# Pair products on one core: weight loads by the software queue alternate between 14 and 15 DMA engines, dealt from one place further on

## The chip, the cores and the metric

The kernel runs on one core of a Trainium2 chip. The metric is the device time of one execution in microseconds (us): the median of the runs shown, and beside it one execution taken with the hardware profiler.

## The reference

An input x has 1024 rows, 32 fields and 128 values a field; there is one 128 x 128 weight matrix for each of the 496 pairs of fields i < j. For each pair, field i's values go through the pair's matrix, and the result is multiplied, element by element, with field j's values:

```python
v_i = inputs[:, I_IDX, :]
v_j = inputs[:, J_IDX, :]
transformed = jnp.einsum('bpd,ped->bpe', v_i, W)
return transformed * v_j
```

All is float32. The output has 1024 x 496 x 128 elements, 260 MB; the inputs are 49 MB together. So the kernel writes five times what it reads.

## The kernel before

The 496 pairs are worked off in one order, written out by hand in the loop of line 300: each step u is a half pair, 512 of the 1024 rows. Pairs stand from the last first field to the first, so that fields are needed one after the other. The order in the program is the order on each engine; there is no scheduler.

For a half pair, TensorE makes two products (line 268) of a split of x and of the weights into parts with fewer bits, ScalarE scales the sum (line 270), TensorE adds a third product (line 279), and VectorE multiplies with the other field from PSUM into an output slot (line 244). The first 15 pairs use plain float32 products (line 265). Weights are split in chunks of two pairs by `split_w` (lines 149 to 153: ScalarE, then three GpSimd instructions), x by `split_x`.

Stores are issued on ScalarE's queue (line 318), three or four pairs at a time, 1.5 or 2 MB in rows of 12 or 16 KB per partition. `slots` has room for 12 pairs; until the x fields that need it are loaded, the room of those fields holds output too (`ot`). VectorE has to wait for a slot's store to be done before it writes there again.

Weights come in tiles of eight pairs, 128 partitions x 4 KB = 512 KB, 62 of them. Three tiles have room at a time; when the last chunk of a tile is split, the loop (line 324) loads the tile three further on into its place. SyncE issues most of the loads (line 132). From tile 12 on, every second tile (`WAPART`: 12, 14, ... 60, 25 tiles) is loaded in two parts by `load_apart`:

- the first 112 partitions by the software queue, issued on GpSimd (line 114). The source is written as 14 x 8 rows, and the host has laid the tile's rows out in that order, so that the DMA falls into 14 pieces of eight rows of 4 KB;
- the last 16 partitions by SyncE (line 115), a row for each of the 16 DMA engines.

`move_on(k)` (line 111) is a DMA of the same software queue that reads 2k rows of 64 bytes as k pieces into a tile, `mark`, that nobody reads. It is called with 5 once before the loads begin (u = 30), with 16 - 14 = 2 three pairs after each load (`BACK`), and with 13 after the last one. The numbers sum up to 5 + 25 x 14 + 24 x 2 + 13 = 416 = 26 x 16.

Of the kernel before, what the change touches and what calls it, by code (L numbers as in the profile page):

```python
# [11 lines left out]
P = 128  # L12
# [5 lines left out]
WL = 8  # L18
# [12 lines left out]
XLEAD = 5  # L31

XG = 4
NE = 14
ROWS = 8 * NE
WAPART = tuple(range(12, 62, 2))
BACK = 3
FOURS = 73
NS = 12
# [18 lines left out]
def kernel(  # L58
# [22 lines left out]
    nc = tc.nc  # L81
# [12 lines left out]
    def load_x(f, pieces=1, eng=None):  # L94
        if f == 0:

            t = rpool.tile([P, WL, P], F32, tag="w", name="x_0").rearrange("p q e -> p (q e)")
        else:
            t = xpool.tile([P, BT], F32, tag=f"x{f}", name=f"x_{f}")
        s = BT // pieces  # L100
        for k in range(pieces):
            (eng or nc.sync).dma_start(out=t[:, k * s : (k + 1) * s], in_=xt[f, :, k * s : (k + 1) * s])
        x_sb[f] = t

    w_raw = {}
# [3 lines left out]
    def move_on(k):  # L109

        nc.gpsimd.dma_start(out=mark[: 2 * k], in_=xt[0, : 2 * k, :16].rearrange("(b a) n -> a b n", a=k))

    def load_apart(dst, src):
        nc.gpsimd.dma_start(out=dst[:ROWS], in_=src[:ROWS].rearrange("(b a) m n -> a b m n", a=NE))
        nc.sync.dma_start(out=dst[ROWS:], in_=src[ROWS:])

    group = {}

    def load_group(k, m):
        if m == XG - 1:  # L120
            group[k] = xpool.tile([P, XG, BT], F32, tag=f"g{k}", name=f"x_g{k}")
        f = XG * k + 1 + m
        x_sb[f] = group[k][:, m, :]
        nc.sync.dma_start(out=x_sb[f], in_=xt[f])

    def load_w(c, splits=(0, WL), eng=nc.sync):
        w_raw[c] = rpool.tile([P, WL, P], F32, tag="w", name=f"w_{c}")
        if c in WAPART:
            load_apart(w_raw[c], wt[c])
            return  # L130
        for a, b in zip(splits, splits[1:]):
            eng.dma_start(out=w_raw[c][:, a:b, :], in_=wt[c, :, a:b, :])
# [59 lines left out]
    todo.sort(key=lambda t: t[1])  # L192

    load_w(0, (0, 1, WL), nc.sync)
    load_x(NF - 2, pieces=2, eng=nc.scalar)
    load_x(NF - 1, pieces=2, eng=nc.scalar)
    load_x(NF - 3)
    load_x(NF - 4)
    load_w(1, eng=nc.sync)
    for f in range(NF - 5, NF - 4 - XLEAD, -1):  # L200
        load_x(f)
    load_w(2, eng=nc.sync)


# [3 lines left out]
        if c < WRING:  # L208
            w_at[max(c * WL - 3 * WC + 1 - WLEAD, free)] = c

    back = []
    last = NQ // WL
    ring = [*range(WRING - WB, XAFTER + 1), "x", *range(XAFTER + 1, last)]

# [42 lines left out]
    def first(u):  # L257
        q, h = divmod(u, 2)
        i, c = pairs[q][0], q // WC
        r = slice(q % WC * P, (q % WC + 1) * P)  # L260
        s = slice(h * HB, (h + 1) * HB)
        if h == 0:
            po[q] = po_t[q % PB]
        if q < nq0:
            nc.tensor.matmul(po[q][:, s], w_raw[q // WL][:, q % WL, :], x_sb[i][:, s], start=True, stop=True)  # L265
        else:
            for t in (0, 1):
                m = nc.tensor.matmul(po[q][:, s], w_s[c][t][:, r], x_s[i][t][:, s], start=t == 0, stop=t == 1)  # L268
                apart(m, scaled.get(u - 1) if h else None)
            scaled[u] = nc.scalar.mul(po[q][:, s], po[q][:, s], 1.0 + EPS)  # L270
            apart(scaled[u], taken.get(q - PB), "TensorE's products, which this waits for, have waited for it")

    def second(u):
        q, h = divmod(u, 2)
        i, j = pairs[q]
        r = slice(q % WC * P, (q % WC + 1) * P)
        s = slice(h * HB, (h + 1) * HB)
        if q >= nq0:
            m = nc.tensor.matmul(  # L279
                po[q][:, s], w_s[q // WC][2][:, r], x_s[i][2][:, s], start=False, stop=True, skip_group_check=True  # L280
            )
            apart(m, scaled[u ^ 1])
        g, k = group_of[q]
        if k == 0 and h == 0:
            ots[g] = out_tile(g)
        if q >= NQ - 2:
            write(g, k, s, po[q][:, s], x_sb[j][:, s])
        elif h == 1:
            taken[q] = write(g, k, slice(0, BT), po.pop(q), x_sb[j])
        ot = ots[g][0]  # L290
        n = groups[g][1]
        if q >= NQ - 2:
            stores.append((u + SLAG, rows(g)[:, k, s], ot[:, k, s]))
        elif g in (0, len(groups) - 1):
            if h == 1:
                stores.append((u + SLAG, rows(g)[:, k], ot[:, k]))
        elif k == n - 1 and h == 1:
            stores.append((u + SLAG, rows(g), ot))

    for u in range(2 * NQ + LAG + SLAG):  # L300
        q = u // 2
        if u < 2 * NQ:
            i, j = pairs[q]
            if u % 2 == 0 and j == i + 1 and XG * ngroup < i - 2 - XLEAD:
                load_x(i - 2 - XLEAD)
            first(u)
            if u == 2 * nq0:
                move_on(5)
            if u % 2 == 0 and q in group_at:
                load_group(*group_at[q])  # L310
            if u % 2 == 1 and q in w_at:
                load_w(w_at[q])
            if u % 2 == 0 and q in back:
                move_on(16 - NE if max(w_raw) < WAPART[-1] else 13)
        if LAG <= u < 2 * NQ + LAG:
            second(u - LAG)
        while stores and stores[0][0] <= u - LAG:
            nc.scalar.dma_start(*stores.pop(0)[1:])
        if u % 2 == 1:
            ready = [t for t in todo if t[0] <= q]  # L320
            if ready:
                ready[0][2](u)
                todo.remove(ready[0])
        if ring[WB:] and ring[0] in spent:
            ring.pop(0)
            c = ring[WB - 1]
            if c == "x":
                load_x(0)
            else:
                load_w(c)  # L330
            if c in WAPART:
                back.append(q + BACK)
        while later and later[0][0] <= u:
            nc.vector.tensor_tensor(*later.pop(0)[1:], ALU.subtract)  # L334
    assert not todo and not later and not stores
# [31 lines left out]
```

## Time and profile before

| | |
|---|---|
| median of three runs | 746.08 us (744.96 to 748.08) |
| the profiled execution | 741.81 us |
| its span, first to last instruction | 739.9 us |
| busy: PE / DVE / ACT / POOL | 703.9 / 637.3 / 634.0 / 595.0 us |
| mean granted TensorE clock | 0.989 |
| moved by DMA | 310.02 MB, mean 419 GB/s |
| store of 1.5 MB, of 2 MB from `slots`, issue to landing | 12.6, 16.5 us |
| software load of 448 KB, issue to landing | 11.6 us |
| SyncE's 64 KB of the same tiles | 6.0 us |

PE is TensorE, DVE VectorE, ACT ScalarE, POOL GpSimd and SP SyncE. The profile's page gives busy time by engine and by line, 40 equal slices of the span with the share of time that the 16 DMA engines were busy, the DMA queues (q10 carries what ScalarE issues, q1 what SyncE issues, q0 the software queue), and who waited for whom. A line such as "A <- B: 29.6, 30, 6.2" says that A waited for B for 29.6 us in all, 30 times, 6.2 us at the longest. The trace behind it has every DMA packet with its queue, start, duration and size, but not the engine that moved it.

### The profile page before, as it was taken

The numbers are of one execution on the slowest core, as the hardware profiler recorded it, in microseconds if no ns is written. First come the engines' busy times: TensorE is split into PE (matmuls) and PEld (weight loads), VectorE is DVE, ScalarE is ACT, GpSimd is POOL, SyncE is SP. The second block draws the span as 40 slices with busy tenths as digits, with TensorE's granted clock in tenths as the row PEclk, the third lists the DMA queues.
The fourth block names the chain that finished last, engine by engine and source line by source line (L and its number), as shares of the span: only waits on it lengthen the run. The fifth ranks groups of instructions, "written<-read, shape, count | busy, mean of one in ns | idle before, by whom it ended". The sixth has DMA issues, their size and how long they took to land.

```text
span 739.9 us, 10346 instructions
## 1 busy us (share of the span) xinstructions
PE 703.9 (95%) x2946; PEld 550.4 (74%) x2946; DVE 637.3 (86%) x550; ACT 634.0 (86%) x1256; POOL 595.0 (80%) x882
## 2 busy tenths in 40 slices
PE   7999999999999999999899979999999999999994
PEld 3577777878778888776688758886778887777782
DVE  3898999999999999988798868987999988997884
ACT  1298999999999999998899968998989999898892
POOL 1789999999999999987789776988787888797660
PEclk9999999999999999999999999999999999999997
DMA  9999999999999999999999999999999999999998
GB/s 346 422 429 423 430 413 429 426 418 428 423 421 428 421 426 424 427 418 426 425 427 424 428 425 406 419 424 425 424 425 419 423 421 421 426 416 424 423 430 330
DMA packets 36968, 310.02 MB, mean 419 GB/s; under 512 B 5552, under 2 KB 5680, under 8 KB 19120
## 3 DMA queue, kind: packets, MB, share of 16 engines
q10 hardware_dynamic: 21888, 261.11, 83.6%
q1 hardware_dynamic: 10592, 36.77, 12.4%
q0 software_dynamic: 4432, 11.48, 4.0%
q8 instruction: 24, 0.39, 0.2%
q14 instruction: 32, 0.26, 0.1%
HBM read 49.29 MB, written 260.05 MB: 418 GB/s over the span
## 4 chain that ended last, share of the span: by engine, by line
PE 60%; DMA 22%; DVE 8%; POOL 3%; ACT 3%; issue 2%; ACTq 0%; DVEq 0%; POOLq 0%
PE po L268 38%; DMA out_dram<-slots 20%; PE po L279 18%; DVE slots L244 5%; PE po L265 4%; ACT po L270 2%; DVE xd L334 2%; DMA out_dram<-ot 1%; DVE ot L244 1%; POOL wd L153 1%; POOL wl L151 1%; POOL xl L168 1%; DMA x<-in_xt_dram 1%; POOL xl L169 0%; POOL wd L152 0%
## 5 line engine op out<-in xcount | busy, mean ns | idle before, releaser
L270 ACT ACTIVATE po<-po 128x512 f32<-128x512 f32 x962 | 553.3, 584 | 74.0 <-PE po L268 57.4
L268 PE MATMUL po<-xh,wh 128*128 128x512 f32 x962 | 382.0, 397 | 17.3 <-DVE slots L244 15.2
L279 PE MATMUL po<-xd,wd 128*128 128x512 f32 x962 | 376.4, 391 | 4.8 <-DVE xd L334 2.4
L268 PE MATMUL po<-xl,wl 128*128 128x512 f32 x962 | 377.2, 392 | 1.2 <-POOL wl L151 0.9
L244 DVE TENSOR_TENSOR slots<-po,x 128x1024 f32<-128x1024 f32 (+1 forms) x263 | 314.0, 1213 | 56.3 <-DMA out_dram<-slots 21.1
L268 PEld LDWEIGHTS po<-xh,wh 128*128 128x128 f32 x962 | 181.2, 188 | 74.0 <-DVE slots L244 30.8
L151 POOL TENSOR_TENSOR wl<-w,wh 128x256 fp32r<-128x256 f32 x241 | 184.8, 767 | 63.6 <-ACT wh L149 57.9
L279 PEld LDWEIGHTS po<-xd,wd 128*128 128x128 f32 x962 | 181.2, 188 | 45.0 <-DVE slots L244 3.2
L268 PEld LDWEIGHTS po<-xl,wl 128*128 128x128 f32 x962 | 181.3, 189 | 40.7 <-POOL wl L151 3.9
L153 POOL TENSOR_TENSOR wd<-wl,wd 128x256 fp32r<-128x256 f32 x241 | 180.3, 748 | 20.1
L244 DVE TENSOR_TENSOR slots<-po,x_g 128x1024 f32<-128x1024 f32 x123 | 148.4, 1223 | 22.3 <-DMA out_dram<-slots 8.5
L244 DVE TENSOR_TENSOR ot<-po,x 128x1024 f32<-128x1024 f32 x99 | 119.4, 1221 | 13.6 <-PE po L279 2.6
L152 POOL TENSOR_SCALAR wd<-wh 128x256 fp32r<-128x256 f32 x241 | 103.5, 429 | 20.5
L149 ACT ACTIVATE wh<-w 128x256 fp32r<-128x256 f32 x241 | 98.6, 410 | 5.7 <-DVE slots L244 5.7
L334 DVE TENSOR_TENSOR xd<-xh,xl 128x512 fp32r<-128x512 f32 x52 | 48.0, 924 | 0.0
L168 POOL TENSOR_TENSOR xl<-x_g,xh 128x512 fp32r<-128x512 f32 x32 | 41.6, 1300 | 2.2 <-ACT xh L167 2.0
L168 POOL TENSOR_TENSOR xl<-x,xh 128x512 fp32r<-128x512 f32 x20 | 25.8, 1292 | 15.8 <-ACT xh L167 15.6
L169 POOL TENSOR_SCALAR xl<-xl 128x512 fp32r<-128x512 f32 x52 | 34.4, 662 | 4.6
L265 PE MATMUL po<-x,w 128*128 128x512 f32 x60 | 29.5, 650 | 4.1 <-DMA x<-in_xt_dram 4.1
L265 PEld LDWEIGHTS po<-x,w 128*128 128x128 f32 x60 | 12.1, 207 | 20.7 <-issue 14.5
L167 ACT ACTIVATE xh<-x 128x512 fp32r<-128x512 f32 x20 | 12.3, 624 | 11.5 <-DMA x<-in_xt_dram 11.4
L167 ACT ACTIVATE xh<-x_g 128x512 fp32r<-128x512 f32 x32 | 20.0, 624 | 0.0
(8 smaller groups left out, 49.5 us busy)
## 6 DMA issues: line engine op xcount, KB each, us to landing
out_dram<-slots ACTq DMA_DIRECT2D x67, 1536.0 KB, 12.6
out_dram<-slots ACTq DMA_DIRECT2D x44, 2048.0 KB, 16.5
out_dram<-ot ACTq DMA_DIRECT2D x28, 2048.0 KB, 12.7
w<-in_wt_dram SPq DMA_DIRECT2D x36, 512.0 KB, 10.9
w<-in_wt_dram POOLq DMA_DIRECT2D x25, 448.0 KB, 11.6
x_g<-in_xt_dram SPq DMA_DIRECT2D x16, 512.0 KB, 16.3
x<-in_xt_dram SPq DMA_DIRECT2D x14, 512.0 KB, 9.4
out_dram<-slots ACTq DMA_DIRECT2D x5, 512.0 KB, 8.9
```

The source lines that it names most:

```text
L149: halved[c] = nc.scalar.mul(h, raw, 1.0 - 2.0**-13)
L151: nc.gpsimd.tensor_tensor(l, raw, h.bitcast(F32), ALU.subtract)
L152: nc.gpsimd.tensor_scalar(d, h.bitcast(F32), EPS, 1.0, ALU.mult, ALU.mult)
L153: nc.gpsimd.tensor_tensor(d, l.bitcast(F32), d.bitcast(F32), ALU.subtract)
L168: nc.gpsimd.tensor_tensor(l, x_sb[f][:, s], h.bitcast(F32), ALU.subtract)
L169: nc.gpsimd.tensor_scalar(l, l.bitcast(F32), 1.0 / EPS, 1.0, ALU.mult, ALU.mult)
L244: i = nc.vector.tensor_tensor(ot[:, k, s], p, f, ALU.mult)
L265: nc.tensor.matmul(po[q][:, s], w_raw[q // WL][:, q % WL, :], x_sb[i][:, s], start=True, stop=True)
L268: m = nc.tensor.matmul(po[q][:, s], w_s[c][t][:, r], x_s[i][t][:, s], start=t == 0, stop=t == 1)
L270: scaled[u] = nc.scalar.mul(po[q][:, s], po[q][:, s], 1.0 + EPS)
L279: m = nc.tensor.matmul(po[q][:, s], w_s[q // WC][2][:, r], x_s[i][2][:, s], start=False, stop=True, skip_group_check=True)
L334: nc.vector.tensor_tensor(*later.pop(0)[1:], ALU.subtract)
```

## The change

The tiles loaded apart alternate: 12, 16, ... keep 14 pieces by the software queue, and 14, 18, ... take 15 pieces of eight rows (120 partitions). A 14-tile's last 16 rows still come by SyncE with the load. A 15-tile's last eight rows come by the software queue too, written as eight rows of two halves, at the place of the mark (`load_rest`, three pairs later), and ahead of it. The mark after a load moves on by 16 less the pieces of the next load (1 or 2), after the last by 12; the first mark has 6 instead of 5. The sum is 6 + 13 x 14 + 12 x 15 + 12 x 1 + 12 x 2 + 12 = 416 again, without the eight-row DMAs.

```diff
-NE = 14
-ROWS = 8 * NE
-WAPART = tuple(range(12, 62, 2))
+WAPART = {c: 14 + k % 2 for k, c in enumerate(range(12, 62, 2))}
+WLAST = max(WAPART)
...
-    def load_apart(dst, src):
-        nc.gpsimd.dma_start(out=dst[:ROWS], in_=src[:ROWS].rearrange("(b a) m n -> a b m n", a=NE))
-        nc.sync.dma_start(out=dst[ROWS:], in_=src[ROWS:])
+    def load_apart(c):
+        n = WAPART[c]
+        dst, src = w_raw[c], wt[c]
+        nc.gpsimd.dma_start(out=dst[: 8 * n], in_=src[: 8 * n].rearrange("(b a) m n -> a b m n", a=n))
+        if n == 14:
+            nc.sync.dma_start(out=dst[8 * n :], in_=src[8 * n :])
+
+    def load_rest(c):
+        if WAPART[c] == 15:
+            a, b = [t[120:].rearrange("a (b m) n -> a b m n", b=2) for t in (w_raw[c], wt[c])]
+            nc.gpsimd.dma_start(out=a, in_=b)
+        move_on(12 if c == WLAST else 16 - WAPART[c + 2])
...
             if u == 2 * nq0:
-                move_on(5)
+                move_on(6)
...
             if u % 2 == 0 and q in back:
-                move_on(16 - NE if max(w_raw) < WAPART[-1] else 13)
+                load_rest(back[q])
...
             if c in WAPART:
-                back.append(q + BACK)
+                back[q + BACK] = c
```

On the host, the rows of a 15-tile are laid out for 15 x 8 instead of 14 x 8.

## The prediction

> **What bounds the kernel now.** I read the page's slices first, then the busy time by stretches, then the queues and the waits.
>
> ```profile
> DMA  9999999999999999999999999999999999999998
> q10 hardware_dynamic: 21888, 261.11, 83.6%
> q1 hardware_dynamic: 10592, 36.77, 12.4%
> q0 software_dynamic: 4432, 11.48, 4.0%
> ```
>
> All 40 slices have the DMA engines at 90% or more, and the three queues sum to 100.0% of 16 engines: the output (q10) takes 84%, the loads by SP (q1) 12%, the software queue (q0), which the change touches, 4%.
>
> ```profile
> 20.00:126.00 106.00, 101.81 (x407) 75.29 (x405) 97.11 (x85) 85.09 (x172) 93.20 (x128) 1.00 1.01 426
> 126.00:697.00 571.00, 554.81 (x2379) 444.17 (x2380) 502.76 (x433) 517.46 (x1028) 480.95 (x720) 0.99 1.01 423
> 697.00:728.00 31.00, 29.80 (x131) 24.01 (x129) 26.91 (x24) 27.50 (x54) 16.93 (x27) 1.00 1.00 426
> 728.00:740.00 12.00, 1.52 (x3) 0.58 (x3) 2.61 (x5) 0.00 (x0) 0.00 (x0) 0.61 0.70 283
> ```
>
> The columns are busy time of PE, weight load, DVE, ACT and POOL, granted clock, DMA share and GB/s. From 20 to 728 us the DMA share is full; compute ends at 732.1, and the last 6 us are stores alone. PE's 95% are stretched by waits for room:
>
> ```profile
> DVE slots L244 <- DMA out_dram<-slots: 29.6, 30, 6.2
> PEld po L268 <- DVE slots L244: 30.8, 40, 5.8
> PE po L268 <- DVE slots L244: 15.2, 18, 5.4
> POOL wl L151 <- ACT wh L149: 57.9, 66, 8.0
> PEld po L268 <- POOL wl L151: 3.9, 8, 1.2
> ```
>
> DVE waits for stores to leave their slots, and PE for DVE. So a store counts as gone when its slowest DMA engine is done, and the time is the work of the DMA engine that has most of it. That needs the engines one by one. The trace's packets carry no engine number, but an engine starts its next packet about 4 ns before the one ahead ends (a 16 KB packet takes 611 ns and the next starts 607 after it), so packets can be strung into 16 chains. Where two chains end within a few ns they may swap names, so I use a chain only for some 16 us around each software load. Three readings:
>
> 1. From 20 to 728 us the 16 chains are idle for 22 engine-us of 11,328: nobody has slack, and who gets 1 us more ends 1 us later. Their last packets end between 735.3 and 738.5 us, 736.4 in the mean.
> 2. In the 17 loads where it can be read cleanly, two chains have no 4 KB packet of q0, only one-row and 4-byte ones, and the following mark DMA falls on just these two. The marks' 128-byte packets (66 = 5 + 24 x 2 + 13) say the same: a software DMA of k pieces uses k engines in turn, and the next goes on behind. Counted from where the kernel begins, the first mark takes engines 0 to 4, each load 5 to 15 and 0 to 2, and each small mark 3 and 4. Engines 3 and 4 are passed over 25 times.
> 3. These two are the slow ones. One (A) needs 25 to 50 ns more than 611 for nearly every 16 KB store from 30 us on, that is 33 ns lost per us, before any weight load by software, and about 0.49 us more around each load. The other (B) loses nothing before 126 us, and then 1.23 us around each load (stores of 700 to 760 ns instead of 611), in two bursts: while the software load runs and at the start of SP's next one. The 14 others lose about 0.13 us a load. I can't tell which of 3 and 4 is A.
>
> Being passed over pays for this: a load costs a taking engine 8 rows and one of SP's 16, 9 x 155 = 1.40 us net; a passed one a row and 8 small packets, 155 + 8 x 5 = 0.20. The difference, 1.20 us a load, 30.0 us in all, meets A's loss (33 ns x 710 us + 25 x 0.49 = 35.7 us) and B's (25 x 1.23 = 30.8), against some 3.3 for the others plus instruction fetches.
>
> **The change part by part.** Load number 1, 3, ... (13 of them) stay at 14 engines; 12 go to 15. Starting at 6 instead of 5, a 14-load takes 6 to 15 and 0 to 3 and passes 4 and 5; one place on, a 15-load takes 5 to 15 and 0 to 3 and passes only 4. So 4 is passed over always, 5 thirteen times, and **3 never**. A 15-load costs a taker 8 rows and one 2 KB piece, 8 x 155 + 80 = 1.32 us, a passed one 0.12. Over 25 loads (before: takers 34.9, passed 4.9 us):
>
> - engine 3: 13 x 1.40 + 12 x 1.32 = 34.0, so +29.1 us
> - engine 4: 13 x 0.20 + 12 x 0.12 = 4.0, so -0.9 us
> - engine 5: 13 x 0.20 + 12 x 1.32 = 18.4, so -16.5 us
> - the 13 others: 34.0, so -0.9 us
>
> The bytes are the same, so nothing is won in the sum; 29 us of one engine are shared out among others that can't use them, since a store waits for the last engine. Engine 3 is A or B, and ends now at about 735 to 736 us by its place among the store landings before 700 us (both at or up to 2 us ahead of the median). With 29.1 more it ends at 764 to 765 instead of 738.5: **+26 us**, if it stays as slow as it is. If the added slowness around a load comes from being passed over, an engine that takes part loses 0.13 instead of 0.49 (A) or 1.23 (B): A gives back 9 us, ending at +17; B 27.5, leaving +1.6 on an engine that has as much slack. No row shows a slow engine taking part, so these are the two ends.
>
> Small edits: 12 more DMA issues on POOL at 632 ns (row L111) are 7.6 us, hidden in POOL's 57.9 us of waiting for ACT above; uncovered, they would lengthen the 3.9 us that PE waits for POOL, at most to 11.5. SP drops 12 issues of 327 ns, off the path. The last 8 rows of a 15-tile now come behind the mark's place, 2.7 us after the load's issue (149.03 and 151.69), and land at most 13.2 us later (longest mark); the tile is split 18 pairs, about 26 us, after its load, so 10 us cover it. Uncovered, ACT's split would wait, with the scaling of products queued behind it and PE behind that. The extra halves of rows (96 packets more at 5 ns) are nothing. The 12 new software DMAs of 0.6 us themselves might each start a burst as a load does; at 1.23 us on one engine that is up to 15 us more on a slow one, which the top of the range takes in part.
>
> [...] The 66 packets show k engines for k pieces when k is the outermost size. [...] No run here shows a k of 1.
>
> **The rivals.** *B is engine 3 and is slow only because it is passed over.* For it: B loses nothing in 96 us before the first software load. Against it: B's second burst comes during SP's ordinary load, in which it is not passed over; and other engines that wait for their turn in a load lose 3 to 20 ns a store where B loses 50 to 120. Then B's +1.6 is covered, all others save 0.9, and the time is 744 to 747, the same.
>
> *Faster.* The same mechanism at its limit: engine 3 is B and gives back all of its 27.5 us, which over 16 engines is 1.7 us, and engine 3's turn in the loads evens out the ends (last 738.5, mean 736.4) for up to 2.1: 3.8 us, 742.3. It decides only if engine 3 gives back 27 of its 29 us or more; each us short of that, past its slack, is a us on the end.
>
> *The place doesn't move as written* (a mark of 1 takes two engines): 3 never, 4 only once passed over; both slow engines carry 28 to 29 us more: 771 to 775.
>
> **How the numbers follow.** The profiled execution took 741.81 us with a span of 739.9, and the median shown is 746.08; I add differences to the median. Forecast, engine 3 left without cover: between +17 (A, giving back) and +26 (A or B as now), nearer to the second, which is how both behave in every row: +24, **770 us**. Chances: as now 0.42, A giving back 0.15, drift 0.09, so slower 0.66; the same 0.28; faster 0.06. A measurement of this kernel tells about 0.5%, 3.7 us, from no change. The range runs from 744 (the same, with its gain of 2 us) to 775 (drift, or a few bursts more); little over 1 in 10 lies outside. The slower case alone: 762 to 775.
>
> **What would show it.** Right: the DMA share falls below 1.00 between 126 and 697 us, to about 0.97, GB/s from 423 to some 410; waits of DVE for out_dram grow from 29.6 by about 20 us; landings of a store stretch, one engine ending it alone by several us; the last stores trail on one engine. Wrong: the share stays at 1.01 with 423 GB/s and the chains still end within 4 us; then B was slow by being passed over. The drift would show in mark packets: q0 has 6 + 12 + 24 + 12 = 54 packets of 128 bytes if a mark of 1 takes one engine, and 42, with 24 of 64 bytes beside them, if it takes two.

## The result, and the profile after

The changed kernel takes **758.0 us** (median of 4 runs, 757.05 to 758.37) where the kernel before takes 745.52 (4 runs, 743.99 to 748.08): ratio **1.0163**, interval 1.0126 to 1.02. (A ratio here is that of the record's comparison of runs in the same state, and not exactly the quotient of two medians.) It is slower, as forecast, but by 12.5 us and not by 24. The profiled execution took 757.05 us, its span is 755.2; against the profiled execution before that is 15.2 us more.

The page's slices and queues, after:

```profile
DMA  9999999999999999999999989999999999999996
q10 hardware_dynamic: 21888, 261.11, 82.5%
q1 hardware_dynamic: 10208, 35.98, 12.0%
q0 software_dynamic: 4816, 12.27, 4.4%
```

The DMA engines are still the bound. The last slice is new: 6 where there was an 8. By stretches (busy PE, weight load, DVE, ACT, POOL, granted clock, DMA share, GB/s):

```profile
20.00:126.00 106.00, 101.90 (x409) 75.51 (x408) 97.29 (x85) 85.64 (x172) 93.39 (x129) 1.00 1.01 427
126.00:697.00 571.00, 545.86 (x2319) 432.71 (x2318) 488.44 (x423) 505.29 (x1002) 478.23 (x717) 0.99 1.00 414
697.00:728.00 31.00, 30.28 (x133) 24.52 (x132) 26.35 (x23) 27.86 (x56) 20.68 (x33) 1.00 1.00 417
728.00:740.00 12.00, 12.00 (x54) 9.94 (x53) 10.78 (x10) 10.85 (x21) 5.64 (x9) 1.00 0.93 384
740.00:756.00 16.00, 2.35 (x8) 1.06 (x7) 4.14 (x6) 1.37 (x3) 0.00 (x0) 0.71 0.56 226
```

Until the first software load (126 us) nothing has changed. From then to 697 us the rate falls from 423 to 414 GB/s. The share of 1.00 in this row is a mean over 571 us, and hides a stretch in which the engines stand idle. From 440 to 455 us, first before, then after:

```profile
440.00:455.00 15.00, 13.27 (x47) 10.77 (x48) 11.68 (x11) 9.26 (x18) 6.08 (x11) 0.77 1.00 406
440.00:455.00 15.00, 9.06 (x34) 7.07 (x33) 7.03 (x7) 6.58 (x13) 6.72 (x11) 0.77 0.75 306
```

Here the stores go over from four pairs to three, and in both kernels VectorE waits over 6 us for a slot; for 11 to 12 us no store is issued (434.3 to 445.6 us before, 441.8 to 453.6 after). The trace has 16 landings for each store. Before, half of those of the store issued at 429.0 us have come 14.7 us later, and the last 1.5 us after that: the engines have work for the gap. After, half of those of the store issued at 430.7 have come 8.0 us later, and the last 9.8 us after that: most engines run dry, and 0.25 x 15 = 3.75 us of each engine's time are lost in the mean. The last landing of a store trails the median by up to 10.6 us ahead of the gap, by 3.9 behind it, then by up to 7.7 again; before, by 3.0 at most.

Past 728 us the share falls again. The stores issued from 728 us on land on 15 engines within 0.1 us or so of their median, except one or two, and on one engine 4.5 to 5.8 us later; from 749.9 to 753.5 us a single engine works. (Before, the 16 ended between 735.3 and 738.5.) Idle engines are not all: the packets from 20 us on take 11,689 us of engine time in place of 11,578, 7 us for each engine. Part of that lies in the executions compared: the one before is near the fast end of its kind (see e12 below).

The waits:

```profile
POOL wl L159 <- ACT wh L157: 65.6, 70, 8.2
PEld po L276 <- DVE slots L252: 39.7, 55, 6.4
DVE slots L252 <- DMA out_dram<-slots: 30.9, 31, 6.8
PE po L276 <- DVE slots L252: 18.9, 22, 5.9
DVE ot L252 <- DMA out_dram<-ot: 7.2, 4, 4.6
PEld po L276 <- POOL wl L159: 5.8, 10, 1.2
```

And before, beside the lines shown in the prediction:

```profile
DVE ot L244 <- DMA out_dram<-ot: 2.1, 4, 0.9
```

VectorE waits 1.3 us more for stores out of `slots` (29.6 before) and 5.1 more for `ot` (2.1). TensorE's waits for VectorE's slots grow by 8.9 (30.8) and 3.7 (15.2). Most of the time, then, VectorE hardly feels an engine that trails by 5 to 10 us. The lag is paid where the other engines have run out of stores: in the gap at 440 us, and at the end.

**The place drifts.** q0's mark packets are 42 of 128 bytes and 24 of 64, the number that the forecast named for a mark of 1 that takes two engines. Strung into chains as in the prediction, the first loads read so (A is the chain that loses some 20 ns on nearly each 16 KB store):

- load 1, 14 pieces: A and one neighbour have no 4 KB packet. The 64-byte packets of the mark behind it are not on these two but on two chains that took part with eight rows.
- load 2, 15 pieces and eight rows: A has nine rows. The next mark of 2 falls on A and one other chain.
- load 3, 14 pieces: these two are passed over. The 64-byte packets are on the same two chains as in load 1.
- from load 4 on, A has eight or nine rows wherever the chains can be read; the passed-over chains are others.

That fits this reading: the two-row mark and the eight rows are dealt from the same first engines each time (0, 1 and 0 to 7) and leave the place alone; e9 below tests it. The eight rows go as eight packets of 4 KB: q0 has 2,992 of them, 13 x 112 + 12 x 120 + 12 x 8, and none of the 2 KB halves that the kernel writes. Each pair of loads then moves the place by 14 + 15 + 2 = 31, one back from where it was. The 14-loads pass over engines 4 and 5, then 3 and 4, then 2 and 3, and so on round the ring; **engine 4 is passed over in 2 loads of 25**, engine 3 in 3.

### The profile page after: what moved, and what is told of

Read it like the earlier page. It is cut to its first block, busy times and chain, and to the rows that moved or that the text cites. A ratio compares the mean times of both kernels' runs of the same rounds, so it can differ in the third digit from the quotient of the medians.

```text
span 755.2 us, 10345 instructions
## 1 busy us (share of the span) xinstructions
PE 708.6 (94%) x2946; PEld 550.2 (73%) x2946; DVE 635.3 (84%) x550; ACT 635.0 (84%) x1256; POOL 602.2 (80%) x894
## 4 chain that ended last, share of the span: by engine, by line
PE 55%; DMA 26%; DVE 9%; POOL 4%; issue 3%; ACT 2%; ACTq 0%; DVEq 0%; POOLq 0%
PE po L276 34%; DMA out_dram<-slots 22%; PE po L287 17%; DVE slots L252 6%; PE po L273 4%; DMA out_dram<-ot 3%; DVE xd L342 2%; ACT po L278 2%; DVE ot L252 1%; POOL wl L159 1%; POOL xl L176 1%; POOL wd L161 1%; DMA x<-in_xt_dram 1%; POOL xl L177 0%; POOL wd L160 0%
## 5 line engine op out<-in xcount | busy, mean ns | idle before, releaser
L161 POOL TENSOR_TENSOR wd<-wl,wd 128x256 fp32r<-128x256 f32 x241 | 183.0, 759 | 20.1
L176 POOL TENSOR_TENSOR xl<-x,xh 128x512 fp32r<-128x512 f32 x20 | 25.8, 1291 | 15.5 <-ACT xh L175 15.2
L273 PEld LDWEIGHTS po<-x,w 128*128 128x128 f32 x60 | 11.9, 205 | 20.2 <-issue 14.4
## 6 DMA issues: line engine op xcount, KB each, us to landing
out_dram<-slots ACTq DMA_DIRECT2D x67, 1536.0 KB, 13.2
w<-in_wt_dram SPq DMA_DIRECT2D x36, 512.0 KB, 10.6
```

What stands on the lines that cost most here:

```text
L161: nc.gpsimd.tensor_tensor(d, l.bitcast(F32), d.bitcast(F32), ALU.subtract)
L176: nc.gpsimd.tensor_tensor(l, x_sb[f][:, s], h.bitcast(F32), ALU.subtract)
```

## The experiments

The theory after the result is T: engine 4 alone is slow of its own, engine 3 only while it is passed over, and the drift leaves engine 4 uncovered. Its first rivals are R1, engine 3 is slow of its own as forecast, and R2, the added small DMAs cost the time; both are told in the first expectation.

Times are medians; the kernel before took 744.93 (e1 to e4), 747.9 (e5 to e8), 746.87 (e9 to e11), 747.03 (e12, e13) and 747.38 us (e15, e16) in the same comparisons. Where store losses are told "a load", they are what the 16 and 12 KB stores of one chain take above 611 and 460 ns in the 18 us around a software load, over the loads in which chain A can be told. "Slow stores" are the 16 and 12 KB stores of the whole execution that lose 60 to 400 ns. Both are estimates from one execution of each kernel.

### Which engine needs cover: e1, e2

```diff
-                move_on(5)
+                move_on(6)    # e1; last mark 12.   e2: move_on(4), last mark 14
```

> The kernel before with only the place moved on by one (first mark 6, last 12): all 25 loads pass over engines 4 and 5, engine 3 takes part in all. Theory T (engine 4 is slow chain A and slow of its own, 33 ns per us; engine 3 was chain B and slow only while it was passed over; in the changed kernel the two-row mark lets the place drift, so that engine 4 is passed over in 2 loads of 25 and ends alone): A is covered, 744 to 748 us, the bursts move from engine 3 to engine 5. Rival R1 (engine 3 is slow of its own, as forecast): +17 to +26, 762 to 772. Rival R2 (the 12.5 us of the changed kernel come from its 12 more marks and 12 small software DMAs, not from who is passed over): no new DMA here, 744 to 748, and then the next runs decide.

Measured: **746.29 us, ratio 1.0001** (0.9967 to 1.0035). Engine 3 now takes part in all 25 loads, and the time stays. The chain passed over beside A loses 0.54 us a load there, the ones that take part 0.10. R1, which is the forecast, is out.

> The kernel before with the place one back (first mark 4, last 14): all loads pass over engines 2 and 3, engine 4 takes part in all. T: engine 4 carries 27.5 us more and gives back some 9 that it lost around loads while passed over, so it ends at 753 to 755 instead of 735 to 736: +14 to +17, 759 to 763 us, one engine trailing alone. R1 with engine 3 as chain A: 3 stays covered and 4 is B, +0 to +26. R2: no change, 744 to 748.

Measured: **759.67 us, ratio 1.0172** (1.0132 to 1.0213): as much as the whole change costs, from moving the place back by one. Engine 4 is A. Its windows show the same pattern as the changed kernel:

```profile
126.00:697.00 571.00, 544.79 (x2307) 430.15 (x2306) 484.50 (x421) 503.44 (x997) 468.23 (x702) 0.99 1.00 413
740.00:758.00 18.00, 5.78 (x24) 3.91 (x22) 7.30 (x8) 4.25 (x8) 0.00 (x0) 0.78 0.68 277
```

413 GB/s at a mean share of 1.00 (0.83 from 440 to 455 us), then a tail.

### No cover at all, and what taking part costs: e4, e8

```diff
-WAPART = tuple(range(12, 62, 2))
+WAPART = ()          # e4: all tiles by SP
```
```diff
-NE = 14
+NE = 16              # e8: 25 loads of 16 pieces by the software queue, no marks between
```

> The kernel before with no load by the software queue: all w tiles by SP over 16 engines, no marks but the first. T: engine 4 has an equal share and its own slowness, 753 to 755 at its end, +13 to +17, 758 to 763 us, about as the changed kernel; the 15 others end earlier than in any other run, as no engine is passed over, and no store of an engine other than 4 shows a burst. R1: the same or more. R2: none of the small DMAs, 744 or below.

> The kernel before with its 25 loads by the software queue dealt to all 16 engines, 8 rows each, no marks between, nothing by SP. Engine 4 has its equal share, as in e4_sp_only, but takes part in software loads. T with A giving back (an engine that takes part loses 0.13 us a load): 754.5 of e4 and up to 3.3 us more, 754 to 758 us. Rival (engine 4 loses 0.49 us around each software load whether it takes part or not, as the forecast's +26 assumed): 764 to 767 us.

Measured: e4 **754.47 us, 1.0103** (1.0063 to 1.0143), below the 758 to 763 that was expected; e8 **754.72 us, 1.0086** (1.005 to 1.0123). Equal, within what can be told (the intervals are some 3 us to either side, and an engine as slow in the loads as when passed over would have cost 9 to 12 us more). So an engine 4 that takes part in software loads loses nothing further around them that shows. The chains say the same: A loses 0.55 us a load in e8 (15 loads, 0.02 of it in slow stores), 0.54 in e2 (12) and 0.55 in the changed kernel (15), about the 33 ns per us that it always loses; passed over, it lost 0.87 in before (18 loads, 0.41 in slow stores). A gives back 0.32 us for each load in which it takes part.

The changed kernel is 3.5 us slower than e4, which spares nobody. The drift and the eight rows explain 1.4: engine 4 has 11 x 8 + 12 x 8 + 12 rows of the eight-row DMAs + 13 of SP's = 209 rows there and 200 in e4, at 155 ns. The rest stays open; it is no more than the intervals of the two ratios leave.

### The change without the drift: e3, e5

```diff
-        move_on(12 if c == WLAST else 16 - WAPART[c + 2])
+        for k in (12,) if c == WLAST else (2,) if WAPART[c] == 15 else (5, 12):
+            move_on(k)           # e5: the mark of 12 writes a second tile
```

> The changed kernel with the mark of 1 replaced by two marks of 5 and 12, which together move the place by 17, so by 1: engine 4 is passed over in all 25 loads, engine 5 in 13, as the change says. One more mark DMA per pair of loads than in the changed kernel. T: engine 4 is covered, 743 to 748 us. R1: engine 3 uncovered, +17 to +26, 762 to 772. R2: the small DMAs are still there and 12 more, 758 or above.

Measured: **827.76 us, 1.1084**, and for neither theory's reason:

```profile
ACT po L279 <- PE po L277: 145.9, 181, 12.3
POOL mark L110 <- DMA mark<-in_xt_dram: 103.0, 12, 11.2
PEld po L277 <- POOL wl L160: 94.1, 17, 12.4
PE po L277 <- POOL wl L160: 87.1, 13, 12.0
```

Two marks in a row write one tile, so the second waits on POOL until the first has landed, 12 times 8.6 us; the weight splits are queued behind it, and TensorE behind those. The second mark needs a tile of its own:

> As e3_no_drift, but the mark of 12 goes to a tile of its own, so that POOL does not wait for the mark of 5 to land (103 us of waits in e3). The place then moves by 1 as the change says: engine 4 passed over 25 times, 5 13 times. T (only engine 4 needs cover; the drift is what cost 12.5 us): 743 to 748 us. Rival R2 (the small software DMAs cost by themselves; here 24 more marks than before and the 12 last rows): 755 to 765 us.

Measured: **742.27 us, ratio 0.9929** (0.9889 to 0.9969). With the place where the change says it is, the kernel is **faster than before**. Its waits:

```profile
PEld po L281 <- DVE slots L257: 29.4, 43, 5.4
DVE slots L257 <- DMA out_dram<-slots: 23.3, 28, 5.8
...
DVE ot L257 <- DMA out_dram<-ot: 1.4, 2, 0.9
```

VectorE's waits for stores are down to 23.3 us. R2 is out too: the kernel has 38 marks where before has 26 (12 more, the expectation miscounts them as 24) and the 12 small DMAs. The loss of the changed kernel goes with the drift. The gain is another matter: e12 and e16 below get as much from one more small DMA alone, which e5 has too.

### What moves the place: e6, e9, e10

```diff
+            nc.gpsimd.dma_start(out=mark[:17], in_=xt[0, :17, :16])      # e6, for the mark of 1
```

> The changed kernel with the mark of 1 made of 17 rows instead of 2; 17 has no divisor from 2 to 16. [...] If the small mark does not move the place for another reason (it is dealt from a fixed engine), the drift stays: 755 to 760 us. [...]

Measured: **757.51 us, 1.0113** (1.0075 to 1.0151), the drift. Each of the 12 marks has eight packets of 128 bytes and one of 68: two rows on each of eight engines and one on a ninth. A is passed over in load 1 and has nine rows in load 2.

```diff
-                    move_on(2)
+                    nc.gpsimd.dma_start(out=mark[:2], in_=xt[0, :2, :16])     # e9, in the kernel before
```

> The kernel before with its 24 small marks of 2 pieces of 2 rows each replaced by 2 plain rows (2 x 16 numbers, no outer dimension of pieces). Theory D (a software DMA of plain rows is dealt from a fixed engine and leaves the place where it is): each load of 14 then moves the two passed engines back by two, engine 4 is passed over in loads 1, 9, 17 and 25 only, and the time is that of an uncovered engine 4: 753 to 758 us. Rival (the two rows take two engines at the place and move it by two, as the forecast's drift has it): nothing changes, 743 to 748 us.

Measured: **755.2 us, 1.0133** (1.0087 to 1.018), with nothing changed but the form of the marks. The chains show the two passed over moving back by two a load, and A among them in loads 1 and not in 2 to 4; the 64-byte packets are on the same two chains in loads 1, 2 and 3. Plain rows don't move the place: D holds.

So in the forms that were run, plain rows take the same engines each time, by the chains and packets: two rows take two (e9), the eight rows of the changed kernel eight (96 packets of 4 KB in 12 DMAs), 17 rows nine (e6, eight packets of 128 bytes and one of 68).

```diff
-        move_on(12 if c == WLAST else 16 - WAPART[c + 2])
+        move_on(12 if c == WLAST else 17 if WAPART[c] == 14 else 2)      # e10; 17 pieces of 2 rows
```

> The changed kernel with the mark of 1 replaced by one mark of 17 pieces of 2 rows. [...] Rival (17 is dealt out over 9 engines or from a fixed place): the drift stays or becomes another, 752 to 759 us.

Measured: **755.45 us, 1.0127** (1.0067 to 1.0186), in the rival's range but not for its reason. Each such mark is one packet of 2176 bytes (34 x 64) on one engine and 15 of 136 bytes on the others, so 17 pieces do take one engine, and A is passed over in all 10 loads in which it can be told, and takes part in none. The place is right and the kernel is slow all the same: the slow stores lose 107 engine-us, where e5 has 37 (the profiled execution is the slowest of the four, 758.78 us), and one part of each store again lands up to 8.5 us behind the median. Why these marks do that, and on which engine, is not shown; the packets themselves sum up to 0.7 us an engine.

### Passing over engine 4 alone, and who loses in bursts: e7, e11, e12, e13, e15, e16

```diff
-NE = 14
+NE = 15             # rest by SP; marks of 5 and 12 after each load (e7), one of 17 x 2 rows (e11)
```

> The kernel before with all 25 loads of 15 engines, marks of 5 and 12 after each (place on by 17), the last 8 rows by SP: only engine 4 is passed over, always. T: engine 4 is covered as before, and no other engine has bursts (25 x 1.23 us of engine 3 in before, 1.9 us over 16 engines): 741 to 746 us, at most 0.5% faster than before. R2: 25 more marks, 755 or above. If SP's 8 rows fall on 8 fixed engines these get 3.9 us more than the others: 746 to 749.

> As e7_only15, with one mark of 17 pieces of 2 rows in place of the marks of 5 and 12. If it moves the place by one: engine 4 alone passed over, with 25 marks fewer, 740 to 744 us. If it does not move the place: engine 4 passed over in 2 loads of 25, 753 to 757 us.

Measured: e7 **742.36 us, 0.9905** (0.9875 to 0.9935), the lowest ratio of all, though e12's below lies in its interval; A loses 0.84 us a load, all others 0.04. That SP brings the last eight rows, whichever engines take them, costs nothing that shows. e11: 762.03 us, 1.0236 (1.0163 to 1.0309), outside both expectations; engine 4 is covered in all 11 loads that can be read, and the slow stores lose 131 engine-us.

So e7's gain could be that engine 3 is no longer passed over (in before it loses 0.89 us a load), or lie in its marks:

```diff
-                    move_on(2)
+                    move_on(9)
+                    move_on(9, mark2)       # e12, in the kernel before: 18 is 2 again
```

> The kernel before with each small mark of 2 replaced by two marks of 9 in two tiles (9 + 9 = 18, place on by 2 as before; engines 3 and 4 passed over as before). 15 descriptors per engine and load in place of 12, as in e7_only15. In before the stores that lose more than 60 ns lose 68 engine-us in all, in e5 and e7 34 to 37, in e8 (nobody passed over) 63, in e10 and e11 107 to 131. Theory P (these losses are those of passed-over ordinary engines): engine 3 is still passed over, 60 to 90 engine-us, 744 to 748 us. Theory Q (they depend on how many descriptors the software queue deals, so on where in its ring each load begins): 30 to 40 engine-us, 740 to 744 us.

Measured: **741.48 us, 0.9917** (0.9884 to 0.9949), the time of Q. Engine 3 is still passed over and still loses 0.87 us a load, so P is right on the engine; but the others lose 0.040 and not 0.073, and the slow stores 53 engine-us, between the two ranges. Two marks alone bring as much as e7, so that e7's gain need not come from its engines.

The figures of slow stores carry less than the times. The kernel before takes anything from 741.5 to 752.7 us in 67 runs; its profiled execution (741.81 us, 68 engine-us) is one of the fastest. e13 and e15 below, which deal the same weights and marks, have 85 and 99 engine-us in executions of 751.91 and 750.28 us. e5, e7, e12 and e16 take 740.9 to 746.1 us in 25 runs. So what one more small DMA does is to keep the slow end away; the fast end was there before.

```diff
-    nc = _bacc.Bacc("TRN2", target_bir_lowering=False, num_devices=1, dynamic_dma_scratch_size=2048)
+    nc = _bacc.Bacc("TRN2", target_bir_lowering=False, num_devices=1, dynamic_dma_scratch_size=1024)  # e13
```
```diff
+                nc.gpsimd.memset(pause, 0.0)                                     # e15, behind each mark
+                nc.gpsimd.dma_start(out=mark2[:16], in_=xt[0, :16, :16])         # e16, behind each mark
```

> The kernel before with half the memory for the software queue's descriptors (1024 in place of 2048 bytes per partition), nothing else. P: no change, 744 to 748 us, bursts of 60 to 90 engine-us. Q: the losses change by a third or more, and the time by 2 to 5 us in either direction.

> The kernel before with a fill of 128 x 384 numbers on POOL behind each mark (about the 0.6 us of one more DMA issue), no packet more. Theory P2 (e12, e5 and e7 gain because the second issue shifts POOL's work by 0.6 us a load): 740 to 743 us. Theory M (the packets of the second mark do it): 744 to 748 us, as before.

> The kernel before with 16 plain rows of 64 bytes by the software queue behind each mark, one row on each engine, the place unmoved. Theory M: 740 to 743 us, as with two marks. P2: the same, as POOL issues it too. If the order or the number of pieces of the marks matters and not one more DMA: 744 to 748 us.

Measured: e13 745.72 us, 0.9986 (0.9949 to 1.0023), no change; e15 747.36, 0.9986 (0.9949 to 1.0023), no change; e16 **742.81, 0.9945** (0.9911 to 0.9979). One more DMA of 16 rows of 64 bytes brings 0.5% of e12's 0.8%, within the intervals the same. POOL's time alone brings none of it (e15's fill took 0.44 us where an issue takes 0.6). Half the scratch size (e13) changes nothing, against Q. How 16 small rows behind a load keep the slow end away stays open.

| kernel | engine 4 passed over | us | ratio |
|---|---|---|---|
| before / e1 | always | 744.9 to 747.9 / 746.29 | 1 / 1.0001 |
| e5 / e7 / e12 / e16 | always, more small DMAs behind the loads | 742.27 / 742.36 / 741.48 / 742.81 | 0.9929 / 0.9905 / 0.9917 / 0.9945 |
| e10 / e11 | always, marks of 17 pieces | 755.45 / 762.03 | 1.0127 / 1.0236 |
| e4 / e8 | never | 754.47 / 754.72 | 1.0103 / 1.0086 |
| e9 | in 4 loads of 25 | 755.2 | 1.0133 |
| e6 / the change | in 2 loads of 25 | 757.51 / 758.0 | 1.0113 / 1.0163 |
| e2 | never, with 14 pieces | 759.67 | 1.0172 |

## Why the prediction was wrong, step by step

- **The direction.** Slower was right, but by luck. The loss that was forecast, of an engine 3 left without cover, did not occur (e1, 1.0001); the one that came, of an engine 4 left by the drift, had been given 0.09.
- **The bound.** Right. The time is that of the DMA engine with most work, and who is passed over decides it: e2 (759.67 us) and e9 (755.2 us) change nothing else.
- **Two slow engines.** Wrong, and the first step that failed. A is slow of its own and is engine 4. B is engine 3 and is slow only while it is passed over; e1 gives it all its rows back at no cost (746.29 against 744.93 us, ratio 1.0001), where the forecast has +17 to +26. That was the rival of "the same", and the two objections that the text held against it did not stand: in e1 the engine passed over in its place has the losses (0.54 us a load). Three readings spoke for it that the text had: nothing before 126 us, losses only around loads, always the chain without rows. A's size was misread too: it loses 33 ns per us, but not by "25 to 50 ns" a store. From 30 to 126 us, 120 of 2,039 16 KB stores (one engine's share is 127) lose 5 to 50 ns, half of them 14 to 28.
- **"3 never" with the place as written.** With the place as written the change would have come out between e5's 742.3 us, which has more marks, and the time of before: the rival of "the same", given 28 in 100, or the "faster" one, given 6. The sums for engines 4 and 5 (-0.9, -16.5) were of the right kind: nobody was left uncovered.
- **The drift.** It came, and the packet count named beforehand shows it (42 and 24). Three things in it were wrong. That a mark of 1 takes the next two engines and so moves the place by two, the term behind the 771 to 775 us, no run shows. What the runs show is its 24 packets of 64 bytes on the same two engines each time, and a place that two plain rows don't move (e9, 755.2 us). The chance of 0.09 was low for a form that no row showed. And its price, 28 to 29 us more on both slow engines, was mis-sized: it took two slow engines, and an engine 4 as slow in the loads as when passed over. Engine 4 has 209 rows in place of 25, 184 x 155 ns = 28.5 us, less 0.9 of small packets, and gives back 23 x 0.32 = 7.4: 20.2 us. The last packet moved by 15.0 us, from 738.5 to 753.5, and engine 4's own, which the prediction put at 735 to 736, by 17.5 to 18.5. Some 2 us of the sum are not accounted for.
- **"+24, nearer to the second, which is how both behave in every row."** This is the term that set the forecast, and it failed. The rows showed how A and B do around a load only while they are passed over; the end of the range at +17, A giving back, is the one that e8 and the chains bear out, though for engine 4.
- **The base.** The sum was made against an execution of 741.81 us and added to a median of 746.08. The kernel before spreads from 741.62 to 749.82 us in the seven runs beside e9 to e11 alone, the changed one from 757.05 to 758.37. From the profiled execution, 741.81 + 17 = 758.8, within 2 us of 757.05; the 4.3 us between execution and median were counted twice.
- **Where it would show.** One engine ending the stores by several us, and trailing at the end: right. GB/s of 410: 414. A share of 0.97 between 126 and 697 us and 20 us more of VectorE's waits: wrong in size, the share was 1.00 in the mean (0.75 from 440 to 455 us) and the waits for stores grew by 6.4. The other engines work on while one lags, until their own queues are empty.
- **Small edits.** Right. TensorE's wait for POOL grew from 3.9 to 5.8 us at the weight loads and from 0.9 to 2.2 at the products, and the eight rows land 9.3 us after their issue (12.6 at most), sooner than the 13.2 that the prediction allowed:

```profile
w<-in_wt_dram POOLq DMA_DIRECT2D x12, 32.0 KB, 9.3
```

  e3 shows what waits on POOL cost where nothing covers them: 103 us of them cost 83 us. That new software DMAs might start bursts, up to 15 us, does not show in e5; e10 and e11 show that they can, with marks of 34 rows.

## What to carry to other kernels

Where a DMA is to move the place from which the next one is dealt to engines, verify each form of it: a mark on two engines moved the place as 2 pieces of 2 rows and left it alone as 2 plain rows, and that was worth 8 us (e9). If one engine is slow, find out which by leaving it uncovered and then its neighbour, one run each; slowness that appears only in the trace of an engine treated differently doesn't tell the engine from the treatment. A share of 1.00 in the mean of a long stretch can hide a short one in which most engines are idle: read it in slices. Make a sum against the execution whose trace it comes from, and look how far that one lies from the median before adding to the median.

## What the runs showed of the hardware that was not expected

- One of the 16 DMA engines, number 4 when the first one that plain rows are dealt to is 0, loses 14 to 28 ns on about half of its 16 KB stores of 611 ns and 5 to 50 on nearly all, from 30 us on and with no software load near; without cover this costs the kernel about 1% (e4). It is the same number on the three chips that the record names for e2 (759.67 us, not passed over), e7 (742.36, always) and e9 (755.2, in 4 loads of 25).
- An ordinary engine that is passed over by a load of eight rows on each of the others loses 0.5 to 0.9 us on its stores around the load, one that takes part 0.04 to 0.14, by the chains of one execution each.
- The software DMAs of plain rows went to the same engines each time: 2 rows to two (e9), 8 rows to eight (the changed kernel), 17 rows as 8 x 2 + 1 (e6). With an outer dimension of 17 pieces, all 34 rows went to one engine and 136 bytes (34 x 4) to each of the 15 others (e10).
- A DMA of 16 rows of 64 bytes behind each load made the kernel 0.5% faster (e16, 742.81 us) and two marks that deal 18 pieces 0.8% (e12, 741.48 us), with the weights and the output moved as before. The highest of their 14 runs is 746.1 us; before goes up to 752.7.
